# One transfer instead of four for regrouped codes, matmuls of ones ahead of the first tile, bias rows spread by a matmul, and a planner that counts transfers in flight

## The chip, the cores and the metric

The kernel runs on one core of a Trainium2 chip. The time is device microseconds (us) of one execution; before the change three runs gave 791.25, 791.26 and 793.4 us, median 791.26. The engines are PE (TensorE, matmuls), DVE (VectorE), ACT (ScalarE), POOL (GpSimd) and SP (SyncE, which here only issues transfers). Each engine works through its own instructions in the order in which the program gives them; between engines they wait for each other on semaphores.

## What is computed

A transformer block on x of 16 batches of 512 rows of 256 numbers. The attention has positive features (a softmax over each head's 16 numbers) and no softmax over the rows, so it is linear; then a layer norm; then a gated feed-forward layer whose inputs, hidden values and weights are rounded to FP4 in blocks of 16; then a second layer norm.

```python
def favor(x):                                   # per head of 16 numbers
    p = exp(x - max(x)); return p / (sum(p) + 1e-6)
q, k = favor(split(x @ Wq + bq)), favor(split(x @ Wk + bk))
v = split(x @ Wv + bv)
a = (q @ k.T) / (sum(q) + 1e-6) @ v             # no mask, 16 heads
x = layernorm(x + merge(a) @ Wo + bo)

def fp4(x):                                     # blocks of 16 along the last axis
    scale = max(max(abs(block)) / 6, 1e-12)
    return GRID[searchsorted(MID, abs(block / scale))] * sign(block) * scale
def linear(x, w): return fp4(x) @ fp4(w).T      # w_gate, w_up: 704x256; w_down: 256x704
h = silu(linear(x, w_gate)) * linear(x, w_up)
x = layernorm(x + linear(h, w_down))
```

## The kernel before

Work is cut into tiles of 128 rows on the 128 partitions. A batch is four tiles, or two pairs; there are 32 pairs. Every step is given to a planner (`Plan`) as an operation with an engine, an estimated duration, a due time and the buffers that it reads and writes. `Plan.order` then plays the program through: of the operations that could start first on some engine it takes the one with the earliest due time, and so writes out the order of every engine's queue by its own estimates. The order is fixed when the program is built; on the chip only the waits move. An instruction that waits holds up everything behind it on its engine.

The steps of one batch, with their lines: `load_x` brings x (L394; L400 for the first batch, in two halves). `project` transposes x on PE (L636), copies the result on ACT (L639), multiplies by Wq and Wk (L778), and DVE adds the biases on the way out (L781) and takes the maximum of each head (L786), which POOL subtracts (L790). `features` takes the exponent (ACT L801), the sums (DVE L803) and their reciprocals (L810, L813, L814), and POOL multiplies (L820). `key_values` sums k over the rows (DVE L829), multiplies k by x (PE L836), that by Wv with the bias of v (L852, L853), masks it by head (DVE L857) and multiplies by Wo (PE L864, copied by ACT L870). `attend` transposes q, adds x and the bias bo on POOL (L885), multiplies (PE L892) and normalises in `norm` (DVE L733, ACT L740 to L755, POOL L746 to L748); the rows go to DRAM.

Per pair of tiles of the feed-forward layer: `quantise` reads the rows back (L910) and makes FP4 codes (`codes`: block maximum L655, scales L659 and L660, division L663, rounding on ACT L666, a shift L668). The codes lie with rows on partitions and the matmul needs features there: DVE transposes blocks of 32 by 32 words (L921 for x, L1002 for h), `regroup` writes them to DRAM in one transfer (L676) and reads them back in four, one for each block of 32 partitions (L681). The scales take a similar way in `spread_scales` (L691, four writes L699, one broadcast read L704). POOL multiplies codes by scales (L929 for x, L1009 for h). `gate_up` is L957 on PE, silu on ACT L962, product on DVE L964, codes again; `down` is L1026 and a second `norm`. The last pair takes no regrouping: DVE multiplies the codes (L977), PE transposes them (L991). The last two pairs are normalised tile by tile (L718 to L725) and stored from SP (L1038).

The weights of the feed-forward layer are rounded once, between the attention steps of the first batches: `weight_scales` (block maxima in one reduction L509, some twelve small DVE operations), `fp4_exact` in 12 chunks (L563 to L584, on DVE, ACT and POOL), `transpose_gate_up` (L597) and `transpose_down` (L620). The gate and up product of the first pair can only follow.

Transfers are issued from SP and ACT. The framework under the kernel keeps eight semaphores for them, in turn, so a transfer is issued only when the one eight places ahead of it has landed. At the start `load_all` issues x's first halves, Wq, Wk, Wv (L461) and the biases (L462), each bias broadcast from DRAM to 128 partitions (128 KB); `load_rest` brings Wo and bo (L465, L466), w_gate and w_up (L471, L474) and w_down (L475). `fill` sets constants on POOL.

Of the kernel before, what the change touches and what calls it, by code (L numbers as in the profile page):

```python
# [8 lines left out]
F32 = mybir.dt.float32  # L9
# [8 lines left out]
P = 128  # L18
# [4 lines left out]

FIRST = 2
# [3 lines left out]
LAG = 0.3  # L28
# [63 lines left out]
class Op:  # L92
    __slots__ = ("eng", "us", "fn", "due", "preds", "succs", "left", "bufs", "new", "start", "end", "table", "port", "name", "at")


class Plan:
# [7 lines left out]
    def op(self, eng, us, due, fn, ins=(), outs=(), holds=(), table=None, port=None, name=""):  # L104
# [3 lines left out]
        o.port = eng == "POOL" if port is None else port  # L108
# [35 lines left out]
    def order(self):  # L144
        free, tables, rings, out = {}, {}, {}, []
        port = 0.0
# [30 lines left out]
        def start(o, at):  # L177
            if o.port:
                at = max(at, port)
            for p in o.preds:  # L180
                at = max(at, p.end + (LAG if p.eng != o.eng else 0.0))
# [20 lines left out]
        while len(out) < len(self.ops):  # L202
# [17 lines left out]
            free[o.eng] = o.end  # L220
            if o.port:
                port = o.end
# [10 lines left out]
            for b in o.bufs:  # L233
                left, end = ends.get(id(b), (b.users, 0.0))
                ends[id(b)] = left - 1, max(end, o.end)
# [10 lines left out]
def t_pe(n):  # L246
    return 2 * (n / 1200.0 + 0.002)


def t_dve(n):  # L250
    return 0.15 + n / 960.0


def t_act(n):
    return 0.16 + n / 1200.0


def t_ts(n):
    return 0.15 + n / 1920.0


def t_pool(n):
    return 0.07 + n / 525.0
# [3 lines left out]
def tile_favor_fp4_block(  # L267
# [55 lines left out]
    def dma(name, us, due, fn, ins=(), outs=(), queue="SP", issue=0.45, holds=()):  # L323

        op(queue, issue, due, fn, ins=ins, outs=outs, holds=holds)
        op("DMA:" + name, us, due, lambda: None, ins=ins, outs=outs)
# [63 lines left out]
    def load_x(b, due):  # L390
        x = buf([TPB, D], "x", 4, f"x_{b}")
        rows = hidden[b].rearrange("(t p) d -> p t d", p=P)
        if b:
            op("SP", 0.1, due, lambda: nc.sync.dma_start(x.tile, rows), outs=[x])  # L394
            op(f"DMA:x{b}" if b < 4 else "DMA", (0, 9.0, 16.0, 18.0, 3.5)[min(b, 4)], due, lambda: None, outs=[x])
        else:

            def halves():
                for p in range(PPB):
                    nc.sync.dma_start(x[:, 2 * p : 2 * p + 2, :], rows[:, 2 * p : 2 * p + 2, :])  # L400

            op("SP", 0.1, due, halves, outs=[x])
            for p in range(PPB):
                op(f"DMA:x{b}{p}", 4.5 + p, due, lambda: None, outs=[(x, p)])
        if b == 1:
            op("SP", 0.1, due, load_rest)
# [3 lines left out]
    b_qkv = const.tile([P, D3], F32, name="b_qkv")  # L410
    w_o = const.tile([P, DC, D], F32, name="w_o")
    b_o = const.tile([P, D], F32, name="b_o")
# [32 lines left out]
    wqkv_in, wo_in = (loaded(n, t) for n, t in (("wqkv", 7.0), ("wo", 14.0)))  # L445
    NGU, NDN = NW * D // F2, DC * FF // F2
    op("DMA:wgu", 16.0, 0.0, lambda: None, outs=[(gu_b, k) for k in range(NGU)])
    op("DMA:wdn", 20.0, 0.0, lambda: None, outs=[(dn_b, k) for k in range(NDN)])
    wguT_b = [Fixed(f"wguT{i}") for i in range(2)]
    wdT_b = Fixed("wdT")  # L450

    def load_all():

        head = [o for o in plan.ops if o.eng == "SP"][:1]
        for o in head:
            for b in o.new:
                b.make()
            o.fn()
            o.fn = lambda: None
        for i, (w, bias) in enumerate(((Wq, bq), (Wk, bk), (Wv, bv))):  # L460
            nc.scalar.dma_start(w_qkv[:, :, i * D : (i + 1) * D], w.rearrange("(c p) n -> p c n", p=P))  # L461
            nc.sync.dma_start(b_qkv[:, i * D : (i + 1) * D], bias.partition_broadcast(P))  # L462

    def load_rest():
        nc.sync.dma_start(w_o, Wo.rearrange("(c p) n -> p c n", p=P))  # L465
        nc.sync.dma_start(b_o, bo.partition_broadcast(P))  # L466
# [30 lines left out]
    def weight_scales(src, src_b, n, at, name, due):  # L497
# [20 lines left out]
        def rest():  # L518
            amax, scale = pb[:, :nb], pb[:, nb : 2 * nb]
            up, hi, lo, inv = (part(i) for i in range(4))  # L520
            for v in iv:
                v.make()
# [595 lines left out]
```

## Time and profile before

| what | value |
|---|---|
| runs | 791.25, 791.26, 793.4 us, median 791.26 |
| span of the profiled execution | 792.0 us, 10915 instructions |
| POOL, largest group | L1009, 124 x 1058 ns, 179.3 us of idle time before it, 101.4 of them for the codes' transfer |
| DVE, largest groups | L964 128 x 515 ns, L655 64 x 893 ns, L663 64 x 886 ns, L781 64 x 681 ns |
| chain that ended last | PE 62%, DVE 12%, DMA 8%, POOL 8%, issue 4%, ACT 4% |
| codes' transfers, time to landing | g_h (384 KB) 2.8 us, hcT (96 KB, four to a pair) 2.4 us, hq from d_h (384 KB) 4.1 us |
| first loads, time to landing | Wq 3.7, Wk 4.6, Wv 8.4, bq 5.7, bk 7.7, bv 7.6, bo 7.0 us |
| DMA engines | 38.0% busy, 89.23 MB; 93% in the first 20 us, 45% from 272 to 620 us |

The span runs from the first to the last instruction of one profiled execution; nothing else of that execution's time is printed, so the span stands for it. Busy times of different engines overlap. In lines of instructions the first number is the start, the second the duration; what stands in brackets is the idle time of the engine before it and what ended it. In grouped lines the numbers after the bar are the total busy time, the mean in ns and the idle time before. "PE" is the matmul, "PEld" the load of its stationary operand. An fp32 matmul is two passes, so the profile counts two matmuls for one in the program.

### The profile page before, as it was taken

The numbers are of one execution on the slowest core, as the hardware profiler recorded it, in microseconds if no ns is written. First come the engines' busy times: TensorE is split into PE (matmuls) and PEld (weight loads), VectorE is DVE, ScalarE is ACT, GpSimd is POOL, SyncE is SP. The second block draws the span as 40 slices with busy tenths as digits, with TensorE's granted clock in tenths as the row PEclk, the third lists the DMA queues.
The fourth block names the chain that finished last, engine by engine and source line by source line (L and its number), as shares of the span: only waits on it lengthen the run. The fifth ranks groups of instructions, "written<-read, shape, count | busy, mean of one in ns | idle before, by whom it ended". The sixth has DMA issues, their size and how long they took to land.

```text
span 792.0 us, 10915 instructions
## 1 busy us (share of the span) xinstructions
PE 768.6 (97%) x3118; PEld 552.5 (70%) x3118; DVE 656.7 (83%) x1340; ACT 416.5 (53%) x893; POOL 455.9 (58%) x602
## 2 busy tenths in 40 slices
PE   7999999989998999999999999999999999999996
PEld 3567657657676777767777777777777777777774
DVE  2998999999888798697697798888878988778784
ACT  2347766868887783544545444444334444344441
POOL 5668788889887755574554435434533543543633
PEclk9999999999999999999999999999999999999998
DMA  9112411211111044404335454554554554464441
GB/s 277 45 55 86 142 53 54 82 60 62 54 53 62 30 129 133 118 37 124 100 112 138 145 171 136 152 149 134 149 154 135 145 149 140 125 179 129 136 130 41
DMA packets 104348, 89.23 MB, mean 113 GB/s; under 512 B 44512, under 2 KB 87904, under 8 KB 104288
## 3 DMA queue, kind: packets, MB, share of 16 engines
q1 hardware_dynamic: 90704, 71.49, 31.8%
q10 hardware_dynamic: 13584, 17.04, 6.0%
q8 instruction: 25, 0.41, 0.2%
q14 instruction: 35, 0.29, 0.1%
HBM read 53.28 MB, written 35.21 MB: 112 GB/s over the span
## 4 chain that ended last, share of the span: by engine, by line
PE 62%; DVE 12%; DMA 8%; POOL 8%; issue 4%; ACT 4%; SPq 2%; ACTq 0%; POOLq 0%; DVEq 0%
PE bank L957 26%; PE bank L1026 14%; PE bank L778 8%; PE bank L892 5%; PE bank L836 5%; POOL hq L1009 3%; DMA out_dram<-y 3%; DVE qk L781 2%; PE bank L636 2%; DVE mx L786 2%; DMA hcT<-g_h 2%; SPq L681 1%; POOL xqT L929 1%; DVE fs L803 1%; PE bank L852 1%
## 5 line engine op out<-in xcount | busy, mean ns | idle before, releaser
L957 PE MATMUL bank<-w_guT,xqT 128*128 128x352 f32 x1024 | 311.3, 459 | 0.0
L957 PEld LDWEIGHTS bank<-w_guT,xqT 128*128 128x128 f32 x1024 | 193.8, 190 | 100.4 <-ACT g L962 0.2
L1009 POOL TENSOR_TENSOR hq<-hcT,hq 128x384 f32<-128x384 bf16 x124 | 127.3, 1058 | 179.3 <-DMA hcT<-g_h 101.4
L1026 PE MATMUL bank<-w_dT,hq 128*128 128x256 f32 (+1 forms) x768 | 173.1, 379 | 1.1 <-DVE r L718 1.1
L1026 PEld LDWEIGHTS bank<-w_dT,hq 128*128 128x128 f32 (+1 forms) x768 | 144.9, 190 | 27.5 <-issue 1.9
L778 PE MATMUL bank<-w_qkv,xT 128*128 128x512 f32 x256 | 120.8, 602 | 3.8 <-DVE qk L781 1.9
L964 DVE TENSOR_TENSOR h<-bank,g 128x352 f32<-128x352 f32 x128 | 65.7, 515 | 50.9 <-ACT g L962 24.1
L962 ACT ACTIVATE g<-bank 128x352 f32<-128x352 f32 x128 | 57.6, 458 | 87.7 <-PE bank L957 77.8
L666 ACT ACTIVATE sq<-h,magic 128x704 f32<-128x704 uint16 x64 | 56.2, 878 | 79.2 <-DVE h L663 78.6
L820 POOL TENSOR_TENSOR qk<-qk,fr 128x512 f32<-128x512 f32 x64 | 67.0, 1073 | 20.5 <-DVE fr L814 18.9
L790 POOL TENSOR_TENSOR qk<-qk,mx 128x512 f32<-128x512 f32 x64 | 67.4, 1068 | 19.2 <-DVE mx L786 19.0
L778 PEld LDWEIGHTS bank<-w_qkv,xT 128*128 128x128 f32 x256 | 46.6, 193 | 45.4 <-issue 35.8
L755 ACT ACTIVATE y<-r,nb_d,rstd_d 128x256 f32<-128x256 f32 x60 | 32.6, 591 | 59.2 <-POOL nb_d L748 59.2
L929 POOL TENSOR_TENSOR xqT<-xcT,xs 128x256 f32<-128x256 bf16 x64 | 46.3, 740 | 27.6 <-DMA d_h<-sT_h 23.4
L836 PE MATMUL bank<-qk,x 128*128 128x256 f32 x256 | 59.7, 387 | 2.1 <-ACT qT L639 2.1
L892 PE MATMUL bank<-M,qT 128*128 128x256 f32 x256 | 59.6, 381 | 1.8 <-ACT M L870 1.8
L655 DVE TENSOR_REDUCE bank<-h 128x44 f32<-128x704 f32 x64 | 57.1, 893 | 1.6
L663 DVE SCALAR_TENSOR_TENSOR h<-h,bank 128x704 f32<-128x704 f32 x64 | 56.7, 886 | 2.1
L836 PEld LDWEIGHTS bank<-qk,x 128*128 128x128 f32 x256 | 49.5, 195 | 12.7 <-ACT qT L639 3.4
L781 DVE TENSOR_TENSOR qk<-bank,b_qkv 128x512 f32<-128x512 f32 x64 | 43.0, 681 | 18.3 <-PE bank L778 17.9
L892 PEld LDWEIGHTS bank<-M,qT 128*128 128x128 f32 x256 | 47.8, 190 | 13.2 <-ACT M L870 3.8
L885 POOL TENSOR_TENSOR xb<-x,b_o 128x512 f32<-128x512 f32 x32 | 41.0, 1285 | 22.8 <-DVE r L733 22.7
(137 smaller groups left out, 1083.3 us busy)
## 6 DMA issues: line engine op xcount, KB each, us to landing
g_h<-hw SPq DMA_DIRECT2D x31, 384.0 KB, 2.8
hcT<-g_h SPq DMA_DIRECT2D x124, 96.0 KB, 2.4
hq<-d_h SPq DMA_DIRECT2D x31, 384.0 KB, 4.1
dx<-x1n ACTq DMA_DIRECT2D x32, 256.0 KB, 2.0
x<-dx SPq DMA_DIRECT2D x32, 256.0 KB, 3.1
x<-_attn_hidden_states_dram SPq DMA_DIRECT2D x15, 512.0 KB, 3.5
out_dram<-y ACTq DMA_DIRECT2D x30, 256.0 KB, 3.3
xs<-d_x SPq DMA_DIRECT2D x32, 128.0 KB, 2.5
```

Source lines behind the costliest of these rows:

```text
L655: op("DVE", t_dve(n), due, lambda: nc.vector.tensor_reduce(amax[:, g], b3(src()), AX.X, ALU.max, apply_absolute_value=True), ins=[src_b], ...
L778: op("PE", t_pe(D2), due, lambda c=c, u=u, pqk=pqk: nc.tensor.matmul(pqk.tile, xT[:, 2 * c + u, :], w_qkv[:, c, :D2], start=c == 0, stop=c ...
L781: op("DVE", t_dve(D2), due, lambda t=t, pqk=pqk: nc.vector.tensor_tensor(qk[:, t, :], pqk.tile, b_qkv[:, :D2], ALU.add), ins=[pqk], outs=[ ...
L790: op("POOL", t_pool(D2), due, lambda g=g: nc.gpsimd.tensor_tensor(qk3()[:, g, :], qk3()[:, g, :], bcast(mx[:, g], HD), ALU.subtract), ins= ...
L820: nc.gpsimd.tensor_tensor(f3, f3, bcast(r[:, t * 2 * H : (t + 1) * 2 * H], HD), ALU.mult)
L836: nc.tensor.matmul(pxk[:, c * D : (c + 1) * D], x[:, t, c * P : (c + 1) * P], qk[:, t, D:], start=t == 0, stop=t == TPB - 1,)
L892: nc.tensor.matmul(pu(pa.tile)[:, u, :], qT[:, 2 * u + c, :], M[:, c, :], start=c == 0, stop=c == DC - 1,)
L957: op("PE", t_pe(F2), due + u * 0.2 * PAIR, lambda c=c, u=u, lo=lo, ps_=ps_: nc.tensor.matmul(ps_[:, :F2], xqT[:, 2 * u + c, :], w_guT[:, c ...
L962: op("ACT", t_act(F2), due, lambda g=g, pg=pg: nc.scalar.activation(g.tile, pg[:, :F2], AF.Silu), ins=[pg], outs=[g], table="silu")
L964: op("DVE", t_dve(F2), due, lambda g=g, h=h, pu_=pu_, k=k: nc.vector.tensor_tensor(h[:, k * F2 : (k + 1) * F2], pu_[:, :F2], g.tile, ALU.m ...
L1009: op("POOL", t_pool(TG * P), d, lambda u=u, c=c: nc.gpsimd.tensor_tensor(hq()[:, u, :, c, :].rearrange("p g (a t) -> p g a t", t=32), hcT. ...
L1026: op("PE", t_pe(D), due, lambda f=f, g=g, c=c, n=n, u=u: nc.tensor.matmul(pu(pd.tile)[:, u, :], hq()[:n, u, g, c, :], w_dT[:n, f, :], star ...
```

## The change

Four things change. (1) `regroup` reads the codes back in one transfer. For that a feature's place is different: in the blocks of 128 words the DVE transpose takes every fourth word (word 4t + q goes to block q) where it took 32 neighbours, so that in DRAM partition and block run together. (2) At the start DVE sets a 128x128 tile to one, and PE does seven matmuls of it, whose result nobody reads. The four biases come as rows of 1 KB into one partition; a matmul with a row of ones spreads them over the partitions in two steps of 512 columns, copied out of PSUM by DVE. All loads of the start are issued from one function in a written order; x of the first four batches is among them. (3) The planner's estimates change: durations, the delay from one engine to the next (0.3 us for all before), the rule that POOL and certain DVE operations exclude each other is gone, and a transfer is now modelled by its issue, by its share of the DMA engines and by the landing of the one eight places ahead. (4) The block maxima of the weights are taken in pieces of 704 numbers, their scales in four planner steps; in `down` the planner puts a pair's second tile after its first.

```diff
+WARM = 7
+AHEAD, AHEAD_AT = 4, 21.0
+X_AT = ((4.3, 6.0), (8.0,), (10.5,), (20.5,))
-LAG = 0.3
+LAG = 0.06
+DRAIN = 0.165
+OVER = {"DVE": 0.083, "ACT": 0.095, "POOL": 0.041}
+LANDED = 0.09
+LAG_PE = 0.15
+LANES, SEND = 8, 0.6
...
         def start(o, at):
-            if o.port:
-                at = max(at, port)
             for p in o.preds:
-                at = max(at, p.end + (LAG if p.eng != o.eng else 0.0))
+                at = max(at, p.end if p.eng == o.eng == "PE" else p.done + (LAG_PE if o.eng == "PE" else LAG))
+            if o.load is not None:
+                for k in range(o.count):
+                    at = max(at, lands[k - LANES] - k * o.us / o.count)
...
-            free[o.eng] = o.end
-            if o.port:
-                port = o.end
+            if o.load is not None:
+                for k in range(o.count):
+                    served = max(served, t + (k + 1) * us / o.count + SEND) + o.load
+                    lands.append(served + SEND)
+                o.landed = lands[-1]
+            elif o.sent is not None:
+                o.end = max(t, o.sent.landed)
+            o.done = o.end + (DRAIN if o.eng == "PE" else LANDED - LAG if o.eng.startswith("DMA") else 0.0)
+            free[o.eng] = o.end - OVER.get(o.eng, 0.0)
...
-    b_qkv = const.tile([P, D3], F32, name="b_qkv")
+    b_all = const.tile([P, D3 + D], F32, name="b_all")
+    b_qkv, b_o = b_all[:, :D3], b_all[:, D3:]
+    b_row = const.tile([1, D3 + D], F32, name="b_row")
+    ones = const.tile([P, P], F32, name="ones")
...
+    def warm(due):
+        pb = psum("pm", "warm")
+        def mm():
+            for _ in range(WARM):
+                nc.tensor.matmul(pb[:, :P], ones, ones, start=True, stop=True)
+        op("PE", WARM * 2 * t_pe(P), due, mm, ins=[ones_b], outs=[pb])
...
     def load_all():
+        nc.vector.memset(ones, 1.0)
...
+        b_in = lambda q, i, v: q.dma_start(b_row[:, i * D : (i + 1) * D], v.unsqueeze(0))
+        half = lambda p: nc.sync.dma_start(xs[0][:, 2 * p : 2 * p + 2, :], rows(0)[:, 2 * p : 2 * p + 2, :])
+        half(0)
+        w_in(nc.scalar, 0, Wq)
+        b_in(nc.sync, 0, bq)
+        w_in(nc.scalar, 1, Wk)
+        b_in(nc.sync, 1, bk)
+        half(1)
+        nc.sync.dma_start(xs[1].tile, rows(1))
+        nc.sync.dma_start(xs[2].tile, rows(2))
+        b_in(nc.scalar, 2, bv)
+        b_in(nc.scalar, 3, bo)
+        w_in(nc.sync, 2, Wv)
         for i, w in enumerate((w_gate, w_up)):
...
+        nc.sync.dma_start(w_o, Wo.rearrange("(c p) n -> p c n", p=P))
         nc.sync.dma_start(dn_raw, w_down.rearrange("(c p) k -> p c k", p=P))
+        nc.sync.dma_start(xs[3].tile, rows(3))
+    def spread_biases(due):
+        for k, b in enumerate((bqk_b, bvo_b)):
+            pb = psum("pm", f"pb_{k}")
+            at = slice(k * D2, (k + 1) * D2)
+            op("PE", t_pe(D2), due, lambda pb=pb, at=at: nc.tensor.matmul(
+                pb.tile, ones[0:1, :], b_row[:, at], start=True, stop=True), ins=[brow_in], outs=[pb])
+            op("DVE", t_dve(D2), due, lambda pb=pb, at=at: nc.vector.tensor_copy(b_all[:, at], pb.tile),
+               ins=[pb], outs=[b])
...
-    def regroup(src, dst, n, tag, name, due):
+    def regroup(src, dst, n, tag, name, due, load):
         d = Buf(dr, [P, 4, n], "g" + tag, 3, f"g_{name}", U32)
-        dma(f"g{name}", 3.0, due, lambda: nc.sync.dma_start(d.tile, src.tile), ins=[src], outs=[d])
-        def back():
-            rows = d.tile.rearrange("(a i) q n -> i a q n", i=32)
-            for q in range(4):
-                nc.sync.dma_start(dst[32 * q : 32 * q + 32, :, :], rows[:, :, q, :])
-        dma(f"h{name}", 3.5, due, back, ins=[d], outs=[dst], issue=1.8)
+        dma(f"g{name}", 2.6 * load, due, lambda: nc.sync.dma_start(d.tile, src.tile), ins=[src], outs=[d])
+        dma(f"h{name}", 4 * load, due, lambda: nc.sync.dma_start(
+            dst.tile, d.tile.rearrange("(a i) q n -> (i q) a n", i=32)), ins=[d], outs=[dst])
...
-            xc.tile.bitcast(U32).rearrange("p (u q t) -> p q u t", u=2, q=4)), ins=[xc], outs=[xw], port=True)
+            xc.tile.bitcast(U32).rearrange("p (u t q) -> p q u t", u=2, q=4)), ins=[xc], outs=[xw])
...
-        op("DVE", t_dve(TPB * D), due, lambda: nc.vector.tensor_reduce(
+        op("DVE", 1.95, due, lambda: nc.vector.tensor_reduce(
             ks.tile, qk[:, :, D:].rearrange("p t d -> p d t"), AX.X, ALU.add), ins=[qk], outs=[ks])
...
-        words = lambda: hc[:, :].bitcast(U32).rearrange("p (u g q t) -> p u q g t", u=2, g=TG, q=4)
+        words = lambda: hc[:, :].bitcast(U32).rearrange("p (u g t q) -> p u q g t", u=2, g=TG, q=4)
...
-                ), ins=[(both, f"{u}{c}{int(g == TG - 1)}"), wdT_b], outs=[(pd, u)], holds=[r], name="down")
+                ), ins=[(both, f"{u}{c}{int(g == TG - 1)}"), wdT_b] + [(pd, 0)] * u, outs=[(pd, u)], holds=[r], name="down")
...
+    warm(due_at(-22))
+    spread_biases(due_at(-20))
```

Some forty other estimates change by a few hundredths to a few tenths of a us in the same way as that of `ks`.

## Prediction

> **What bounds the kernel now.** I read the busy shares of the page first, then the same by stage, then the matmuls one by one.
>
> ```profile
> PE 768.6 (97%) x3118; PEld 552.5 (70%) x3118; DVE 656.7 (83%) x1340; ACT 416.5 (53%) x893; POOL 455.9 (58%) x602
> ```
>
> ```profile
> core 0: us, PE busy (x) PEld busy (x) DVE busy (x) ACT busy (x) POOL busy (x), PEclk, DMA share, GB/s
> 20.00:100.00 80.00, 76.11 (x333) 52.98 (x332) 74.48 (x133) 46.93 (x99) 59.72 (x73) 1.00 0.26 80
> 100.00:200.00 100.00, 95.72 (x418) 66.58 (x417) 95.75 (x179) 71.72 (x154) 84.96 (x106) 1.00 0.19 62
> 200.00:272.00 72.00, 69.57 (x315) 51.30 (x315) 59.24 (x105) 55.94 (x123) 57.76 (x75) 0.98 0.15 50
> 272.00:620.00 348.00, 348.00 (x1375) 253.48 (x1375) 287.34 (x619) 170.00 (x364) 171.70 (x231) 1.00 0.45 130
> ```
>
> Three stages: from 20 to 200 us PE and DVE are both nearly full (DVE 93 and 96%, then 82% up to 272); from 272 to 766 PE is never idle; the last 26 us are a tail. To see what PE could do at best I add its work at the pace of unbroken runs in the chain: L957 9.47 us per 32 matmuls, L1026 5.18 per 24, L778 1.72 per 4, L836 3.45 per 16, L892 1.73 per 8, transposes 0.11 each. Over all 3118 that is 757.4 us. The span of 792.0 so holds 34.6 us of lost PE time: 8.2 before the third batch's first projection (it starts at 24.61 with 16.4 us of work behind it), 17.3 from there to the second pair's gate and up (272.00, work behind it 246.5), none to 766.01, 9.1 after that (26.0 us for 16.9 of work). Only these three losses can change. The timed runs have a median of 791.26, 0.7 below the profiled span; I sum in the span and take 0.7 off at the end.
>
> **Start.** The loads and the first matmuls:
>
> ```profile
> 6.61 8.53 PE L778 MATMUL bank<-w_qkv,xT 128*128 128x512 f32 x16
> ...
> 9.17 0.34 PEld L778 LDWEIGHTS bank<-w_qkv,xT 128*128 128x128 f32 x1 [0.52 <-issue]
> 9.82 0.19 PEld L778 LDWEIGHTS bank<-w_qkv,xT 128*128 128x128 f32 x1 [0.32 <-issue]
> 10.12 0.69 DVE L781 TENSOR_TENSOR qk<-bank,b_qkv 128x512 f32<-128x512 f32 x1 [10.12 <-PE bank L778]
> ...
> 10.26 0.19 PEld L778 LDWEIGHTS bank<-w_qkv,xT 128*128 128x128 f32 x1 [0.24 <-issue]
> ```
>
> x's first tile lands at 4.26, where PE begins. The weight loads come 0.86 us apart up to 9.17 (7.46, 8.31, 9.17) and 0.44 apart from 9.82: PE runs at half pace for its first 5.1 us, though the granted clock of that stage is printed as 1.00. The seven matmuls of ones need only a memset of DVE (0.2 us, by a 128x128 memset on POOL). They start near 1.1 us and take 7 x 2 passes x 0.21 = 3.0 us at half pace (128 of 512 columns of the 0.86 us), done at 4.1, before x at 4.26: they cost nothing. If the pace again doubles 5.1 us after the first matmul, that is at 6.2 instead of 9.4. Behind them stand x's first transposes (4.3 to 5.4) and now two bias matmuls of 512 columns, 2 x 0.86 = 1.7 us at full pace. They run from 5.4 to 7.5, so the first projection starts at 7.5, not 6.61, but ends at 9.3, not 10.0. Its second half ends at 11.0 (11.74 before); then the new order puts two transposes and an eviction wait in (to 12.2), two projections (15.6), two more (19.1), two transposes and a wait (20.2), two more: 23.6 for what starts at 24.61 now, with 0.44 less transposing done. Gain 0.6 us. The bounds: if the pace doubles by 4.3, 1.7 gained; if only at 9.4, 0.9 lost; if the bias rows land as late as the bias broadcasts do now (7.0 to 7.7 us after issue), the second bias matmul holds PE to about 9.5 and 1.5 is lost. I expect them early: they are one row of 1 KB each, behind Wq and Wk on ACT's queue, and Wk lands 4.6 us after 1.32, at 5.9.
>
> [...]
>
> The loads behind: the SP queue stands still from 6.39 + 0.97 to 10.22 because w_gate's tail waits for Wv. In the new order each load waits for one eight places ahead and none of those is a broadcast; w_up can be issued some 2 to 3 us sooner than 11.46 and DVE's first reduction of the weights (19.00, 3.1 us in one piece) comes earlier, in pieces of 0.89. Four pieces and two cost 0.5 + 0.2 us more than the single ones; two bias copies of 0.69 fall into DVE's idle time before 9.3. What the earlier weights are worth is inside the next item.
>
> **Middle, 24.6 to 272.** The planner now has other costs, so every queue is reordered. PE's waits there are short and many:
>
> ```profile
> 42.72 1.13 PE L864 MATMUL bank<-w_o,kvT 128*128 128x256 f32 x4 [1.10 <-DVE kvT L857]
> ...
> 244.08 5.41 PE L836 MATMUL bank<-qk,x 128*128 128x256 f32 x16 [2.08 <-ACT qT L639]
> ```
>
> Each is a matmul standing at the head of PE's queue whose input was planned a little early. The sixteen of 0.4 us or more come to some 14 us, among them 1.8 us of half-pace matmuls after the wait at 244. A plan closer to the rows (evictions 0.165 instead of 0.16, ks 1.95 instead of 1.22, no shared-port rule) should misplace fewer. How many, no row tells. Best case, the kvT, M, qk and qT kind (1.3 + 1.3 + 0.6 + 0.9 + 0.9 + 2.2 + 1.8) goes: 9 gained. Worst case is the third rival, 6 lost. DVE's density leaves little room (at 96% of a 100 us stage there are 4 us), so I take the end nearer to nothing: 2 gained.
>
> **Regrouping.** Per pair the four hcT and four xcT issues (L681, median 0.43 each) become two: SP gets 8 x 0.43 - 2 x 0.43 = 2.6 us back, and the last part lands some 1.3 us earlier. POOL's 101 us of waiting for hcT shrink, but from 272 to 766 PE never waits for POOL, so it is worth nothing there. If the cover were gone, it would be 1.3 us per pair. The price is on DVE: the transposes L921 and L1002 now read every fourth word.
>
> ```profile
> L786 DVE TENSOR_REDUCE mx<-qk 128x64 f32<-128x1024 f32 x32 | 39.0, 1218 | 0.8
> ...
> L1002 DVE STREAM_TRANSPOSE hw<-hcs 128x384 uint32<-128x384 uint32 x62 | 35.4, 574 | 1.2
> L829 DVE TENSOR_REDUCE ks<-qk 128x256 f32<-128x1024 f32 x16 | 31.2, 1949 | 2.0 <-POOL qk L820 2.0
> ```
>
> L829 reads as many elements as L786, but 2 KB apart, and takes 1.69 times as long net of a 0.15 us base. On that row L1002 goes from 0.57 to 0.86 and L921 from 0.44 to 0.64: 2 x 0.29 + 0.2 = 0.8 us per pair. The other bound is nothing: the transposes of the scales (L691) also read with a step and take 0.24 us for 96 words, no more per word than L1002. Either way it is hidden: in 272 to 620 DVE is busy 287.3 of 348, 12.1 of 14.65 us per pair, at most 12.9 afterwards.
>
> [...]
>
> **Tail.** The order after the last gate and up (766.01) changes. Now:
>
> ```profile
> 769.59 5.46 POOL L1009 TENSOR_TENSOR hq<-hcT,hq 128x384 f32<-128x384 bf16 x4 [5.88 <-DMA hq<-d_h]
> ...
> 775.04 3.19 PE L1026 MATMUL bank<-w_dT,hq 128*128 128x256 f32 x14
> ...
> 778.84 6.72 PE L1026 MATMUL bank<-w_dT,hq 128*128 128x256 f32 x30 [0.61 <-DVE r L718]
> ```
>
> PE has little of pair 30 to do until 775.04, since its hq is multiplied from 769.59; that waits for a transfer issued at 764.85, behind four regrouping issues on SP. In the new order the scales' transfer stands ahead of one regrouping issue, so the multiplications can start near 767.7 and pair 30's down starts at once when pair 29's ends. Also hd of the first half now stands before the second half's reduction. Counting from T, the end of gate and up: five down matmuls 2.2; hd at 2.6 (0.4 wait); transposes 0.66; seven down 3.0; five of pair 30 2.2, to 8.5. hd of the second half, by the rows now (0.53 + 0.9 + 0.64 + 0.89 + 0.88 + 1.26 + 1.57 and a copy of 0.42) is ready at T + 8.5 to 9.4. Then 0.66 + 3.0 + 0.35 (the wait on L718) + 5.2: PE ends at T + 18.2, 20.8 now (786.78). The 5.2 us from there to the end are the same work. Gain 2.6, bounds 0 and 3.5.
>
> **Sum.** -0.6 - 2.0 - 2.6 = -5.2: span 786.8, time 786.1; I say 786.
>
> **The rivals.** (1) The middle closes most of its gaps (9 gained): 792 - 0.6 - 9 - 2.6 = 779.8, time 779. For it: so many of the waits are small misplacements. Against: DVE at 96%. (2) The new order does not do better in the middle, and the tail keeps its waits because the two halves still wait on L718: -0.6, time 790.6. (3) Slower: DVE sets the pace until the weights are done. By the order of the instructions with durations of the rows, DVE has 263.1 us of work ahead of the second pair's first product, 265.6 before; PE has only 236.1 of useful work ahead of it, 246.5 before. If DVE decides, that point comes at 272 x 263.1 / 265.6 = 269.5, and PE has 521.3 us left, plus 6.5 of tail loss: 797.3, time 796.6. PE's loss there would be 33.4 us (25.5 now); above 30.5 the kernel is slower by more than 0.3%. For it: DVE's 93 and 96%. Against: by the fifth pair PE's useful work (305.5 against 305.6) and DVE's (320.8 against 319.2) are level again, and DVE has 17% idle there. A seven-matmul warm-up that lifts nothing is inside the start's bounds.
>
> **Chances.** The forecast 0.50, (1) 0.15, (2) 0.15, (3) 0.20. A change within 0.3% (2.4 us) cannot be told from none. Faster by more: 0.46 + 0.15 = 0.61; within: 0.04 + 0.13 + 0.03 = 0.20; slower: 0.02 + 0.17 = 0.19. The forecast's own range is 782 to 790; with the rivals 777.5 to 794.5 leaves out about 2 in 10.
>
> **What would show it.** Matmuls of ones from about 1.1 us and projections 0.43 apart from the first; first DVE bias addition near 9.3; summed PE loss up to the second pair near 23; transposes L1002 between 0.57 and 0.86 us; no PE gap in the steady stage; PE's end 18 us after the last gate and up. I am wrong if PE's loss in the middle grows, or if PE waits for bias rows.

## The result, and the profile after

The changed kernel takes 810.11 us, median of 5 runs (809.06 to 812.21), beside 791.37 for the kernel before on the same chip: 1.0238 of its time, 95% interval 1.0221 to 1.0254. The forecast was 786.0 with a range to 794.5. It is slower, and outside that range. The profiled execution has a span of 808.4 us (792.0 before), so 16.4 us are to be found in it.

The busy shares, then the stages (window; busy time of PE, weight load, VectorE, ScalarE, GpSimd with their instructions; granted clock; DMA):

```profile
PE 779.3 (96%) x3136; PEld 552.6 (68%) x3136; DVE 670.5 (83%) x1347; ACT 416.0 (51%) x893; POOL 458.4 (57%) x602
```

```profile
core 0: us, PE busy (x) PEld busy (x) DVE busy (x) ACT busy (x) POOL busy (x), PEclk, DMA share, GB/s
20.00:100.00 80.00, 78.26 (x342) 54.56 (x341) 78.45 (x150) 50.26 (x106) 62.53 (x77) 1.00 0.25 83
100.00:200.00 100.00, 91.91 (x404) 63.81 (x403) 95.07 (x170) 71.23 (x154) 84.53 (x106) 1.00 0.17 57
272.00:520.00 248.00, 247.42 (x1001) 180.23 (x1000) 199.04 (x413) 123.79 (x260) 124.97 (x166) 1.00 0.39 115
520.00:766.00 246.00, 239.02 (x896) 167.93 (x895) 202.97 (x440) 99.50 (x221) 104.47 (x141) 1.00 0.48 140
```

Up to 100 us PE is busier than before, from 100 to 200 less (91.91, 95.72 before), and in the last row it is not full: 896 matmuls where the kernel before issued 939 in the same 246 us, with VectorE no busier (202.97; 201.78 before). To place the loss I use the prediction's own measure, time minus the matmuls so far at their unbroken pace ("lost time of PE"). Ones and bias matmuls count as work in it, 3.3 us that the kernel before does not have; the last column leaves them out.

| lost time of PE, us | at 25 us | at 300 | 300 to the last gate and up | after that | useful work by 300 |
|---|---|---|---|---|---|
| before | 8.2 | 25.6 | 0.1 | 9 | 274.4 |
| after | 6.3 | 26.0 | 13.6 | 8 | 270.7 |

So 3.7 us of the 16.4 are behind at 300 us (1.4 of them at 25 us already, the 3.3 us of added work counted in), 13.6 come after 300, nearly all after 520 (27.5 lost at 520, 39.6 at the end of the last gate and up), and the tail gives 1.0 back.

**Where PE stops in the steady stage.** PE's instructions in order of time:

```profile
566.95 5.35 PE L1084 MATMUL bank<-w_dT,hq 128*128 128x256 f32 x24
572.14 7.26 PE L1015 MATMUL bank<-w_guT,xqT 128*128 128x352 f32 x24
580.30 1.45 PE L1015 MATMUL bank<-w_guT,xqT 128*128 128x352 f32 x4 [0.90 <-DVE r L791]
582.01 1.45 PE L1015 MATMUL bank<-w_guT,xqT 128*128 128x352 f32 x4 [0.26 <-ACT g L1020]
583.29 5.35 PE L1084 MATMUL bank<-w_dT,hq 128*128 128x256 f32 x24
```

The down product ended at 572.3; r (L791), which reads its bank, frees it only after 579.8, and gate and up of the next tile need it. VectorE in those microseconds:

```profile
573.55 0.69 DVE L717 TENSOR_REDUCE bank<-x 128x32 f32<-128x512 f32 x1 [2.18 <-DMA x<-dx]
...
575.82 0.87 DVE L1060 STREAM_TRANSPOSE hw<-hcs 128x384 uint32<-128x384 uint32 x1
...
578.90 0.65 DVE L725 SCALAR_TENSOR_TENSOR xn<-x,bank 128x512 f32<-128x512 f32 x1
579.47 0.41 DVE L791 SCALAR_TENSOR_TENSOR r<-bank,x 128x256 f32<-128x256 f32 x1
579.81 0.08 DVE L791 DVE_READ_ACCUMULATOR r<-bank,x 128x1 f32 x1
...
580.93 0.89 DVE L1060 STREAM_TRANSPOSE hw<-hcs 128x384 uint32<-128x384 uint32 x1
581.71 0.61 DVE L979 STREAM_TRANSPOSE xw<-xc 128x256 uint32<-128x256 uint32 x1
...
584.86 0.69 DVE L717 TENSOR_REDUCE bank<-x 128x32 f32<-128x512 f32 x1 [1.60 <-DMA x<-dx]
```

VectorE stood for 2.18 us for a reload of x, works from 573.55 without a pause up to 583.26 and reaches r seven microseconds after its input was there; then it stands again, for 1.60 us, for the next reload of x, which went out at 581.86, after r had freed its buffer. What waited in 520 to 766 us (waiting instruction, released by, us, times, longest):

```profile
...
DVE h L1022 <- ACT g L1020: 20.8, 16, 1.9
DVE bank L717 <- DMA x<-dx: 15.4, 12, 3.1
...
PEld bank L1015 <- DVE r L791: 9.9, 10, 2.4
PEld bank L1015 <- ACT g L1020: 8.5, 12, 0.8
```

The same view of the kernel before lists no wait of PE there. VectorE is 83% busy in both kernels; it is not full, but its instructions come late.

**The groups** that answer to those shown before:

```profile
L1067 POOL TENSOR_TENSOR hq<-hcT,hq 128x384 f32<-128x384 bf16 x124 | 125.2, 1040 | 199.6 <-DMA hcT<-g_h 131.9
...
L1060 DVE STREAM_TRANSPOSE hw<-hcs 128x384 uint32<-128x384 uint32 x62 | 54.1, 872 | 0.6
...
L844 DVE TENSOR_REDUCE mx<-qk 128x64 f32<-128x1024 f32 x32 | 38.6, 1207 | 0.2
...
L887 DVE TENSOR_REDUCE ks<-qk 128x256 f32<-128x1024 f32 x16 | 31.3, 1957 | 0.0
```

The reductions are unchanged; the transpose takes 872 ns instead of 574, and the smaller one (L979) 636 instead of 439. GpSimd waits longer for the regrouped codes than before (131.9 us, 101.4 before).

**The start**, PE by time and then its granted clock (the 0.50 before the last two numbers):

```profile
1.10 3.35 PE L484 MATMUL bank<-ones 128*128 128x128 f32 x14 [1.10 <-DVE ones L489]
4.69 0.63 PE L698 MATMUL bank<-ident,x 128*128 128x128 f32 x4 [0.24 <-DMA x<-_attn_hidden_states_dram]
5.25 2.19 PE L525 MATMUL bank<-b_row,ones 1*128 1x512 f32 x4
7.38 5.40 PE L836 MATMUL bank<-w_qkv,xT 128*128 128x512 f32 x8
```

```profile
8.00:9.00 1.00, 1.00 (x3) 0.48 (x2) 0.17 (x1) 0.00 (x0) 0.74 (x1) 0.50 1.05 358
```

The first projection starts at 7.38 as forecast, but eight of its matmuls take 5.40 us (3.70 at full pace, in a run below): 0.24 us in which PE stood between the ones and x were followed by three microseconds at half clock, from 8 to 11.3.

**The tail**, from the last gate and up (L1015) on:

```profile
773.63 9.63 PE L1015 MATMUL bank<-w_guT,xqT 128*128 128x352 f32 x32
783.10 2.32 PE L1084 MATMUL bank<-w_dT,hq 128*128 128x256 f32 x10
786.21 0.94 PE L1049 MATMUL bank<-ident,hd 128*128 128x128 f32 x6 [0.78 <-DVE hd L1035]
...
794.49 6.29 PE L1084 MATMUL bank<-w_dT,hq 128*128 128x256 f32 x28 [0.61 <-DVE r L776]
801.30 1.56 PE L1084 MATMUL bank<-w_dT,hq 128*128 128x256 f32 x6 [0.52 <-DVE r L776]
```

PE ends at 802.86, 19.8 us after gate and up (783.1); before, it took 20.8.

### The profile page after: what moved, and what is told of

It reads as the page before. It is cut to its first block, busy times and chain, and to the rows that moved or that the text cites. A ratio compares the mean times of both kernels' runs of the same rounds, so it can differ in the third digit from the quotient of the medians.

```text
span 808.4 us, 10719 instructions
## 1 busy us (share of the span) xinstructions
PE 779.3 (96%) x3136; PEld 552.6 (68%) x3136; DVE 670.5 (83%) x1347; ACT 416.0 (51%) x893; POOL 458.4 (57%) x602
## 3 DMA queue, kind: packets, MB, share of 16 engines
q1 hardware_dynamic: 87380, 71.22, 30.1%
## 4 chain that ended last, share of the span: by engine, by line
PE 39%; DVE 33%; DMA 9%; issue 7%; POOL 6%; ACT 5%; SPq 2%; DVEq 0%; POOLq 0%; ACTq 0%
PE bank L1015 15%; PE bank L1084 8%; DMA x<-dx 6%; PE bank L836 6%; DVE bank L717 4%; PE bank L894 3%; DVE h L725 3%; PE bank L950 3%; DVE h L1022 3%; DVE r L791 2%; DVE bank L722 2%; DVE hw L1060 2%; DVE mx L844 2%; DVE qk L839 1%; POOL qk L848 1%
## 5 line engine op out<-in xcount | busy, mean ns | idle before, releaser
L1015 PE MATMUL bank<-w_guT,xqT 128*128 128x352 f32 x1024 | 316.6, 461 | 7.0 <-DVE r L791 4.7
L1015 PEld LDWEIGHTS bank<-w_guT,xqT 128*128 128x128 f32 x1024 | 192.0, 190 | 114.8 <-DVE r L791 9.9
L1067 POOL TENSOR_TENSOR hq<-hcT,hq 128x384 f32<-128x384 bf16 x124 | 125.2, 1040 | 199.6 <-DMA hcT<-g_h 131.9
L848 POOL TENSOR_TENSOR qk<-qk,mx 128x512 f32<-128x512 f32 x64 | 67.0, 1070 | 27.5 <-DVE mx L844 27.3
L1020 ACT ACTIVATE g<-bank 128x352 f32<-128x352 f32 x128 | 55.7, 453 | 26.9 <-PE bank L1015 16.9
L987 POOL TENSOR_TENSOR xqT<-xcT,xs 128x256 f32<-128x256 bf16 x64 | 48.5, 777 | 17.1 <-DMA xs<-d_x 10.5
L1060 DVE STREAM_TRANSPOSE hw<-hcs 128x384 uint32<-128x384 uint32 x62 | 54.1, 872 | 0.6
L839 DVE TENSOR_TENSOR qk<-bank,b_all 128x512 f32<-128x512 f32 x64 | 43.0, 680 | 11.1 <-PE bank L836 10.4
L943 POOL TENSOR_TENSOR xb<-x,b_all 128x512 f32<-128x512 f32 x32 | 42.2, 1324 | 10.2 <-DVE r L791 7.1
```

The source lines that it names most:

```text
L848: op("POOL", t_pool(D2), due, lambda g=g: nc.gpsimd.tensor_tensor(qk3()[:, g, :], qk3()[:, g, :], bcast(mx[:, g], HD), ALU.subtract), ins= ...
L1015: op("PE", t_pe(F2), due + u * 0.2 * PAIR, lambda c=c, u=u, lo=lo, ps_=ps_: nc.tensor.matmul(ps_[:, :F2], xqT[:, 2 * u + c, :], w_guT[:, c ...
L1060: op("DVE", 0.15 + TG * P / 960.0, d, lambda u=u: nc.vector.transpose(hw.tile.rearrange("p q (u g t) -> p u q g t", u=2, g=TG)[:, u], word ...
L1067: op("POOL", t_mix(TG * P), d, lambda u=u, c=c: nc.gpsimd.tensor_tensor(hq()[:, u, :, c, :].rearrange("p g (a t) -> p g a t", t=32), hcT.t ...
```

## The experiments

Every ratio is to the kernel before, run on the same chip in turn, with its 95% interval. "Early" is PE's lost time at 300 us, "steady" what it loses from there to the last gate and up, both from the profiled execution. Each profile is of one run, and the runs of one kernel spread by up to 8 us (after_old_margins from 791.26 to 799.24, profiled at 798.17; both_margins_price from 789.06 to 793.98, profiled at 789.65): a difference of a few us between two early numbers means little.

| kernel | ratio | early | steady |
|---|---|---|---|
| after | 1.0238 [1.0221, 1.0254] | 26.0 | 13.6 |
| after_plain_words | 1.0128 [1.0100, 1.0157] | 21.2 | 8.3 |
| before_strided_words | 1.0030 [1.0016, 1.0045] | 24.9 | 0.6 |
| after_priced | 1.0107 [1.0088, 1.0126] | 27.5 | 2.0 |
| half_priced | 1.0088 [1.0056, 1.0120] | 22.5 | 4.3 |
| after_four_reads | 1.0583 [1.0550, 1.0617] | 21.2 | 41.3 |
| after_x_early | 1.0210 [1.0183, 1.0237] | 25.3 | 15.8 |
| priced_one_more | 1.0055 [1.0037, 1.0073] | 25.7 | 1.4 |
| priced_no_ones | 1.0121 [1.0097, 1.0145] | 34.7 | 2.9 |
| priced_four_reads | 1.0139 [1.0100, 1.0177] | 25.7 | 12.7 |
| after_old_margins | 1.0013 [0.9985, 1.0041] | 28.1 | 1.4 |
| after_handover_margin | 1.0164 [1.0139, 1.0189] | 24.7 | 7.0 |
| after_no_overlap | 1.0075 [1.0053, 1.0098] | 26.2 | 0.2 |
| half_margins_price | 1.0057 [1.0035, 1.0078] | 23.6 | 0.3 |
| both_margins_price | 1.0008 [0.9990, 1.0026] | 20.6 | 0.1 |
| both_nudged | 1.0134 [1.0095, 1.0172] | 30.1 | 0.3 |
| before_regrouped | 1.0209 [1.0187, 1.0231] | 40.4 | 2.2 |
| before_start | 1.0357 [1.0316, 1.0398] | 38.7 | 7.1 |
| before_nudged | 1.0229 [1.0188, 1.0271] | 43.4 | 0.1 |

### The strided transposes: taken out, added, and priced

```diff
 # after_plain_words (before_strided_words: the reverse, in the kernel before)
-"p (u t q) -> p q u t"          -"p (u g t q) -> p u q g t"
+"p (u q t) -> p q u t"          +"p (u g q t) -> p u q g t"
```

> The changed kernel with one thing put back: the two transposes of the codes read contiguous words (u g q t and u q t) again. Every queue keeps its order and the regrouping stays one transfer. The features then meet the weights of other features, so what is left of the output is not the reference's; every instruction is there. Theory 1 (the strided transposes: 0.87 instead of 0.57 us and 0.64 instead of 0.44, 0.8 us of VectorE per pair, make VectorE late for the banks in the steady stage): transposes at 0.57 and 0.44, the 12 us that PE loses from 520 us to the last gate and up go down to 0 to 3, time 797 to 801. Theory 2 (the new order is too tight, whatever the transposes take): transposes at 0.57, but the losses stay, 807 to 811. Theory 3 (the one transfer lands later, 4.6 us against 2.4, and what waits for it is late): 808 to 811.

> The mirror: the kernel before with one thing added, the transposes of the codes read every fourth word. Every queue keeps its order and the four regrouping reads stay. The features meet the weights of other features, so the output is not the reference's; every instruction is there. Theory 1: 0.8 us more of VectorE per pair is more than the order before can hide either: PE gaps in the steady stage, 797 to 803. Theory 2: hidden, as the prediction said, 791 to 793. Theory 3: the same, 791 to 793.

Measured: 800.93 us, transposes at 0.57 and 0.42, steady loss 8.3 of 13.6, early loss 4.8 us less (of it 1.8 at 25 us: PE went on to x at 4.32 without a pause, and no half clock came). So of some 11 us between the two profiled spans (9 between the medians) about 5 are the transposes in the steady stage; 3 remain for the dense middle, by subtraction alone. A steady loss of 8.3 stays that theory 1 does not cover (it expected 0 to 3). The mirror takes 793.54:

```profile
L1002 DVE STREAM_TRANSPOSE hw<-hcs 128x384 uint32<-128x384 uint32 x62 | 54.6, 883 | 1.2
```

The same 0.3 us per transpose cost the kernel before 2.3 us, and its steady loss is 0.6. The claim that the work can be hidden was right for the old order; it is the new order that does not hide it.

```diff
 # after_priced (half_priced: 0.53 and 0.71)
-op("DVE", 0.15 + n / 2 / 960.0, due, ... transpose xw      -op("DVE", 0.15 + TG * P / 960.0, d, ... transpose hw
+op("DVE", 0.64, due, ...                                   +op("DVE", 0.87, d, ...
```

> The changed kernel whole, but the scheduler is told what the strided transposes take: 0.87 and 0.64 us instead of 0.55 and 0.42. The order of all queues changes with it. Theory 1 in its form that VectorE's work itself is too much: still 804 to 811. Theory 1 in its form that only the wrong price makes the order wrong: the steady losses go to 0 to 4, 797 to 802. Theory 2: no change beyond the chance of another order, 805 to 812. Theory 3: 808 to 811.

> The changed kernel with the transposes told at half of what was missing: 0.71 and 0.53 us (0.55 and 0.42 in the change, 0.87 and 0.64 in after_priced). Theory Price: about half of the steady loss, 4 to 8 us, time 802 to 806. Theory Tight: the same. Theory Draw: anywhere, outside 799 to 810 too.

Measured 799.39 and 800.9 (half_priced a little under its 802), steady loss 2.0 and 4.3. By price told (0.55, 0.71, 0.87) the steady loss is 13.6, 4.3, 2.0: with nothing changed on the chip but the order, most of it goes.

### The one transfer, and the reload of x

```diff
 # after_four_reads: words as in after_plain_words, told to the scheduler as issue=1.8, count=4
 # priced_four_reads: the same reads, but emitted in the queues of priced_one_more
-nc.sync.dma_start(dst.tile, d.tile.rearrange("(a i) q n -> (i q) a n", i=32))
+for q in range(4): nc.sync.dma_start(dst[32 * q : 32 * q + 32, :, :], rows[:, :, q, :])
```

> The changed kernel with the whole regrouping put back: contiguous words and four reads per regrouping (told to the scheduler as four transfers, 1.8 us of issue); warm-up, biases, loads and scheduler stay changed. The output is the reference's. Theory 1: steady losses 0 to 3, 796 to 801. Theory 2: steady losses stay, 805 to 811. Theory 3: 796 to 801 as for theory 1, and after_plain_words parts the two.

> The queues of priced_one_more, instruction for instruction on PE, VectorE, ScalarE and GpSimd, but with the regrouping of the kernel before: contiguous words, and four reads where one stood on SyncE. The output is the reference's. The scheduler is still told the strided transposes. What differs from priced_one_more is so the 0.8 us of VectorE per pair and six more issues per pair on SyncE. Theory (in the dense middle VectorE's time is PE's time): 2 to 5 us less than priced_one_more, 793 to 796, the transposes at 0.57, PE's loss up to 300 us at 21 to 23 instead of 25.7. Rival (the one transfer is needed in this order: SyncE's 2.6 us more delay what stands behind): 797 to 802.

Both missed: 835.76 and 806.21. With the transposes cheap again, the steady loss is 41.3 and 12.7. In the first, which has another order, PE waited for ScalarE's g, eight times and up to 5.7 us; why this order is so much worse stays open. In the second the four compute queues are those of priced_one_more to the instruction, so the four reads cost 0.84% of the time (1.0139 against 1.0055) although VectorE had 0.8 us less to do per pair. What SyncE waited for longest from 300 to 766 us (L743 are the reads):

```profile
SPq L743 <- DMA out_dram<-y: 72.4, 21, 4.9
```

The read that goes out at 451.91 uses the same of the eight semaphores as a store of y issued at 447.24, which landed at 451.89. In priced_one_more SyncE never waits for a store there; in the kernel before it does (56.3 us, L681), and PE loses nothing by it. Of the chain that ended last, 27% from 520 to 766 us is such landings. So I read the price of the six more transfers per pair as the landings that they had to await, more than as SyncE's time to issue them. The prediction put this at nothing.

```diff
 # after_x_early: bufs + 1 for x1, and in the finished order, for pairs 8 and on
+ops.insert(sp[-5], ops.pop(at))      # the reload of x1, five places earlier on SyncE
```

> The changed kernel with one thing moved: from the ninth pair on, SyncE issues the reload of x1 (L968) five places earlier in its queue, into a seventh buffer instead of the sixth; all other queues keep their order, the transposes stay strided. Theory A (VectorE's 0.8 us more per pair is late by itself): VectorE no longer waits for x, but PE still loses 9 to 13 us from 520 us to the last gate and up, time 806 to 811. Theory B (a loop sets the pace: r of the down product frees x's buffer, the reload starts, VectorE waits for it, and r of the next pair is late): VectorE's waits for x fall from 21 us to under 6, PE's loss there to 0 to 4, time 797 to 803.

Measured 810.15. VectorE no longer waits for x between 520 and 760 us, the steady loss from 520 us on falls from 12.1 to 6.6, but SyncE once stood 6.1 us at a reload whose buffer was not free yet (until 383.57), what is behind it came late, and PE lost 7 us from 408 to 420 us (that the one brought the other is read from the times alone). The reload is a part of the lateness, not its cause, and the run does not price it cleanly.

### The margins of the scheduler

```diff
 # after_old_margins: all four; after_handover_margin: LAG, LAG_PE; after_no_overlap: OVER
 # both_margins_price: all four, on priced_one_more; half_margins_price: half of each
-LAG = 0.06    -LAG_PE = 0.15    -DRAIN = 0.165    -OVER = {"DVE": 0.083, "ACT": 0.095, "POOL": 0.041}
+LAG = 0.3     +LAG_PE = 0.3     +DRAIN = 0.0      +OVER = {}
```

> The changed kernel with four numbers of the scheduler put back: 0.3 us at every hand-over (0.06 and 0.15), no drain (0.165), no overlap of neighbours on an engine (0.083, 0.095, 0.041). The transposes stay strided and told at 0.55 and 0.42. All queues are reordered. Theory Tight (the new order keeps no margin, so a step that takes 0.3 us longer than told is never made up): with the old margins the steady stage loses 0 to 3 us of PE even with the wrong price, time 794 to 801 (the middle may take back some). Theory Price (only the transposes' price matters): steady loss 8 to 14, 806 to 812. Theory Draw (each set of costs gives another order, and how good it is, is chance): no number; any of 795 to 830.

> The changed kernel with the 0.3 us at hand-overs alone put back (0.06 and 0.15 in the change); drain, overlap and the wrong price stay. If the hand-over is the margin that counts: steady loss 0 to 3, time 792 to 799. If the overlap is: 804 to 811.

> The changed kernel with the overlap of neighbours on an engine (0.083, 0.095, 0.041 us per operation) alone set to nothing, so that VectorE is planned some 2.5 us per pair fuller; hand-overs, drain and the wrong price stay. If the overlap is the margin that counts: steady loss 0 to 3, time 793 to 800. If the hand-over is: 804 to 811.

Measured 794.17, 803.21 (between its two ranges) and 796.76. With the wrong price left in, the old margins bring the time back to that of the kernel before:

```profile
520.00:766.00 246.00, 246.00 (x943) 178.67 (x942) 211.61 (x460) 106.80 (x234) 111.33 (x149) 1.00 0.51 146
```

In the stages view of after_old_margins PE is full from 520 to 766 (943 matmuls, 896 in the change) and VectorE does more in the same time (211.61, 202.97). The overlap alone does it for the steady stage (0.2), the hand-over alone does half (7.0). The overlap is what the chip shows, too: above, xn takes 0.65 us (578.90) and r follows after 0.57. A plan that uses it up fills VectorE by 0.083 us at each of its operations, and a step that takes 0.3 us longer than told is then not made up; this last is how I read these runs, no run shows it by itself.

> The changed kernel with the old margins (as in after_old_margins), the right prices for the transposes (as in after_priced) and eight matmuls of ones (as in priced_one_more); the output is the reference's. If price and margin are one cause (slack for VectorE in the steady stage), both together gain nothing over the better of them: 790 to 795. If they are two, the sum: 783 to 788. If too much margin makes the middle loose: 795 to 802.

> The same with half of each margin (hand-over 0.18 and 0.23, drain 0.08, overlap 0.041, 0.047, 0.02). One cause: the steady stage is whole, since the price is right; 789 to 796, between priced_one_more (797.7) and both_margins_price. A dense middle is better packed with less margin, so up to 3 us less than both_margins_price.

Measured 791.53 (12 runs) and 795.01. In the steady stage margin and price fill the same gap: of its 13.6 us the right price alone leaves 2.0, no overlap alone 0.2, all old margins 1.4, both together 0.1. By the whole time it can't be said, since the order of the dense middle changes with each of them by as much (see the smallest edit below). both_margins_price has all parts of the change, with eight matmuls of ones, and the time of the kernel before (interval 0.9990 to 1.0026); no kernel here beat the one before. Half the margin was not better than all of it.

### The start

```diff
 # priced_one_more (on after_priced; the scheduler is told seven)      # priced_no_ones: range(0)
-for _ in range(WARM):
+for _ in range(WARM + 1):
```

> The changed kernel with the right prices for the transposes (as in after_priced) and eight matmuls of ones instead of seven, told to the scheduler as seven, so that no queue changes. Theory (the 0.24 us in which PE stands still between the ones and x, 4.45 to 4.69, brings a stretch of half clock from 8 to 11.3 us): the ones end at 4.9, after x has landed; the granted clock stays at 1.00 from 7 to 12 us, the first eight projections take 3.7 us instead of 5.4, time 797 to 799 against 799.4. Rival (the half clock comes from the bias products or the other executions differ by chance): 0.5 in the windows from 8 to 11 as before, 799 to 801.

> after_priced with the seven matmuls of ones left out and no queue changed (the scheduler is told that they are there). By the prediction's step (0.9 us lost without a doubled pace, 1.7 gained with it): PE begins at 4.3 at half pace, the first eight projections take 5.5 to 7 us, and 1 to 2.5 us are lost against priced_one_more: 798.5 to 801. Rival (the ones bring nothing, since the clock falls again after a gap): 797 to 799.5, as after_priced.

PE's start in priced_one_more, and in priced_no_ones:

```profile
1.10 3.79 PE L484 MATMUL bank<-ones 128*128 128x128 f32 x16 [1.10 <-DVE ones L489]
4.68 1.06 PE L698 MATMUL bank<-ident,x 128*128 128x128 f32 x4
5.67 1.98 PE L525 MATMUL bank<-b_row,ones 1*128 1x512 f32 x4
7.58 3.70 PE L836 MATMUL bank<-w_qkv,xT 128*128 128x512 f32 x8
```

```profile
5.32 3.77 PE L525 MATMUL bank<-b_row,ones 1*128 1x512 f32 x4
9.02 6.25 PE L836 MATMUL bank<-w_qkv,xT 128*128 128x512 f32 x7
```

Measured 797.72, and 803.65 for priced_no_ones, above both of its ranges. With eight, no gap and full pace: eight projections in 3.70 us, ratio 1.0055 instead of 1.0107. Without ones, half pace up to 15 us. In the timed runs no_ones (1.0121) and seven ones (1.0107) are not apart; that the gap behind the seven takes again what they bring is a guess from the starts.

```diff
 # before_start: in the kernel before, ones, bias rows with their matmuls and the new load_all; old scheduler, old costs
+    warm(due_at(-22))
+    spread_biases(due_at(-20))
 # before_regrouped: in the kernel before, the strided words and the one transfer; old scheduler, old costs
+        dma(f"h{name}", 3.5, due, lambda: nc.sync.dma_start(
+            dst.tile, d.tile.rearrange("(a i) q n -> (i q) a n", i=32)), ins=[d], outs=[dst])
```

> The kernel before with the start of the change alone: ones, the bias rows and their two products, the new order of the first loads, under the old scheduler with its old costs. The output is the reference's. By the prediction's step for the start: 789 to 792 (0.6 us gained, bounds -1.7 to +1.5). A rival by the useful work seen at 25 us (1.4 us less than before in the changed kernel): 792 to 795. PE gaps from 300 to 766 us stay at none in both.

> The kernel before with the whole regrouping of the change (every fourth word, one transfer, told to the old scheduler as 0.45 us of issue and 3.5 us of flight, the transposes at the old price) and nothing else. The output is the reference's. Theory A and B: the old estimates leave 3.95 us for a reload that takes 3.1 and 0.3 us at each hand-over, so the regrouping is hidden or nearly: 789 to 796, steady loss under 3 us. A rival (C: the strided read is too dear under any order that counts it at 0.55): 798 to 806 with PE gaps from 520 us on.

Both missed by far: 821.98 and 810.12. From 60 to 260 us PE lost 33.4 and 29.3 us where the kernel before lost 14.7; that is nearly all of the second kernel's loss, and 19 of the 25 us of the first, which loses 7.1 more after 300 us. All of it lies far from the edit of the start. Each part hands the old scheduler other inputs, and it returns another order. That raised the question whether the order before is an ordinary one.

### The smallest edit that reorders

```diff
 # before_nudged (both_nudged: LAG and LAG_PE of both_margins_price)
-LAG = 0.3
+LAG = 0.29
```

> The kernel before with the hand-over told as 0.29 instead of 0.30 us, which reorders all queues and changes no instruction. Theory Draw (the order before is a lucky one): 798 to 825, with the loss between 60 and 260 us and none from 300 to 766. If the parts themselves cost what before_start and before_regrouped showed: 789 to 793.

> both_margins_price with its hand-overs told as 0.29 instead of 0.30 us. If the new costs with the old margins give a good order reliably: 789 to 795, steady loss 0 to 2. If it too is a lucky draw: 797 and more.

Measured 810.71, and 801.78. One hundredth of a microsecond in a planned hand-over, with no instruction changed, costs the kernel before 2.29%, as much as the whole change. Two rows of the stages of before_nudged, and PE in one of its gaps:

```profile
100.00:160.00 60.00, 54.41 (x228) 37.22 (x227) 52.15 (x108) 40.59 (x86) 44.06 (x56) 0.94 0.22 69
160.00:260.00 100.00, 90.53 (x387) 61.72 (x387) 81.18 (x146) 72.15 (x165) 80.49 (x102) 0.98 0.14 49
```

```profile
121.05 8.46 PE L778 MATMUL bank<-w_qkv,xT 128*128 128x512 f32 x12 [2.87 <-ACT xT L639]
```

VectorE is at 87 and 81% there (58.29 of 60 us and 88.14 of 100 in the kernel before): not too much work but the wrong one at the head of a queue. And the gap is paid twice: after 2.87 us of waiting, twelve matmuls take 8.46 us (5.2 at the full pace); the clock of that stage is 0.94, and 0.66 from 120 to 130 us. All three new orders that the old scheduler gave (before_nudged, before_regrouped, before_start) lose 13 to 18 us more by 300 us than the order before, so that one is lucky; both_margins_price lost 9.5 more by its one nudge. The steady stage, on the other hand, loses 0.1 to 1.4 us in all five kernels of the new scheduler with its overlap halved or gone, and 1.4 to 41.3 in the others. The old margins are no warrant: before_start has them, under the old scheduler, and lost 7.1.

## Why the prediction was wrong, step by step

- **What bounds the kernel**: right as a measure; both results can be placed by PE's lost time, stage by stage. But "from 272 to 766 PE is never idle" was read as a property of the stage, and with it "only these three losses can change". It was one of the order.
- **Start (-0.6; 1.4 lost at 25 us)**: times of ones, transposes, bias matmuls and first projection as worked out (4.45, 4.69, 5.25, 7.38; forecast 4.1, 4.3, 5.4, 7.5), bias rows early as expected. What failed is "they cost nothing": x landed 0.24 us after the ones had ended and the half clock followed. The loss is inside the bound of 1.5, but that bound was for late bias rows. Where no gap came (after_plain_words) the loss at 25 us is 4.5, which is 0.4 us gained with the 3.3 of added work. The gap is not the only danger: in after_x_early, with the queues of PE and VectorE as in the change and no gap, the bias matmuls took 3.78 us instead of 2.19, the half pace lasted to 13 us and 7.9 were lost at 25 us. In after_old_margins they took the same 3.78 us.
- **Middle (-2.0, bounds -9 to +6)**: 2.3 us lost, inside the bounds, for a reason the bounds did not hold: orders of this stage differ by some 19 us (early loss 20.6, with 3.5 us of added work besides, to 43.4 over these kernels), and the kernel before stood near the good end.
- **Regrouping (0): the step that failed.** The durations were right at the upper bound (0.87 and 0.64; 0.86 and 0.64 forecast): row L829 was the nearer one, L691 the wrong one. Why a read of every fourth word takes longer (0.87 us against 0.57, 0.64 against 0.44) no run shows. "Either way it is hidden" compared VectorE's 12.9 us with the 14.65 us of a pair. The old order hides it (before_strided_words, 0.6 us of steady loss); the changed one, planned without margin and with 0.55 for 0.87, loses 13.6 in the stage where none was forecast: about 5 by the longer transposes themselves (after_plain_words), the rest by an order made with too low a price and no margin. The cover was a mean over the pair; what counts is how late the one instruction may be that frees a bank. The codes did not come 1.3 us earlier either: from first issue to last landing hcT takes 4.6 us (5.2 before) and xcT 4.7 (3.4), medians of the landings recorded, and GpSimd's wait for hcT grew by 30 us where it was to shrink; PE never waits for GpSimd in this stage. And one transfer in place of four, put at nothing, is worth 0.84% in such an order (priced_four_reads).
- **Tail (-2.6, bounds 0 to 3.5)**: 1.0 gained. GpSimd starts pair 30 at 2.1 us after gate and up (1.7 forecast) and the second half's transposes come at 9.1 (8.5 to 9.4); two waits for L776 behind them (0.61, 0.52; 0.35 forecast) and a longer rest take the other 1.6 us.
- **The rivals**: none. The slower one had VectorE setting the pace "until the weights are done"; the loss came where I had excluded it, after 520 us. Its 265.6 us of VectorE work also added up durations that overlap: in the kernel before VectorE was busy for 238 of the 275 us up to the second pair's first product. The chance I gave to slower (0.19) took the changed costs for better costs. The overlap and the hand-over are closer to the rows, the price of the transposes is not, and the order made from them is worse.

## What to carry to other kernels

Where a program orders all queues from estimates, any edit draws a new order: first find how far the time moves for an edit that does nothing (here a planned 0.30 turned to 0.29 cost 18 us), and hold a forecast against that spread. An estimate that matches the trace need not be the one that plans best: here slack at every operation kept the steady stage full even where a step's price was wrong. Slack only at what frees a shared buffer was not tried. A busy share below full (VectorE 83% here) hides added work only if the instruction that releases the bottleneck (here r, seven microseconds after its input) may come late by as much.

## What the chip showed beyond that

A pause of PE of 0.24 us at 4.45 us was followed by a granted clock of 0.50 from 8 to 11.3 us, in two kernels (after, and after_priced, which has a second pause of 0.11 us); in after_no_overlap a wait of 0.18 us for a bias row was followed by 0.50 to 0.60 from 8 to 11 us and eight projections in 5.40 us instead of 3.70. Of the twelve profiles with ones and no such pause, ten ran at full pace from the first projection on, among them all five with eight ones. Two did not, after_x_early and after_old_margins (here the first):

```profile
5.24 3.78 PE L525 MATMUL bank<-b_row,ones 1*128 1x512 f32 x4
```

There the profile's granted clock reads 1.00 while the pace is half. So the pause goes with one kind of slow start; the other came without any, and what brings it stays open. What makes one order lose 20 us by 300 us and another 43 is left open: the waits seen are for xk, xT, qT and kvT in turn, and no single price or margin was found behind them.
